# Round three's scatters without the copies that tie them to VectorE's newest result

## The chip, the cores and the metric

One core of a Trainium2 chip runs the whole kernel. The metric is the time of one execution on the device, in microseconds (us), as the median of several runs. A profile is one execution more, taken with the hardware profiler; its own time stands beside its span in the table below, since it is not the median.

## The reference, cut to what matters

There are B = 16 graphs of N = 1024 nodes with D = 128 features, and one adjacency matrix for each graph (about 8 neighbours a node). Two residual layers are computed:

```
h = relu(layernorm(x));  x = x + attention(h, adj)            # layer 0
h = relu(layernorm(x));  x = x + gnn(h, dilate(adj))          # layer 1

gnn:   h1 = bn(relu(sage(h,  adj_d, Wr1, Wx1, b1)))
       h2 = bn(relu(sage(h1, adj_d, Wr2, Wx2, b2)))
       h3 = bn(relu(sage(h2, adj_d, Wr3, Wx3, b3)))
       concat(h1, h2, h3) @ Wl + bl
sage:  out = (adj_d @ x / deg) @ Wr + x @ Wx + b;  out / norm(out)
bn:    normalised over all graphs and nodes
```

`dilate` goes through the rows of an adjacency one after another and strikes out neighbours. The batch norm needs sums over all 16 graphs, so each of the three rounds of `gnn` must be over before the next can begin.

## The kernel before, in words

**Stages.** The attention layer and the dilation run together in about the first 785 us of the span, and the dilation ends beside round one. The rows of each graph are written to DRAM in an order of their own there (indirect DMAs on GpSimd into `x2_d`), so that the few nodes that keep neighbours after the dilation stand in the first blocks. Then come three rounds of sage and batch norm over the 16 graphs, called batches here, and a fourth pass that makes the output. Round two ends before 965 us, round three (lines 1305 to 1371) runs from about 985 to 1132.5 us of the span, and round four, the pass that makes the output (lines 1374 to 1439), ends at about 1213 us.

**Order of work.** The program is written out by hand: instructions go to each engine's queue in the order in which Python issues them, and each engine works its queue in order. A `Clock` delays what belongs behind a matmul: `later(n, fn)` issues `fn` n ticks later. `in_turn` (line 1163) takes one piece of a named part, ticks the clock, and calls a function `beside`, which in rounds three and four is `pace_scatters`.

**Round three, for each batch b, in eight ticks** (mix, thirds, mix, mix, thirds, mix, turn, turn; in the last batch the thirds come last):
- `mix` (line 1029) is the sage. PE multiplies into two PSUM halves `po` (lines 1038, 1056, 1063, 1087, 1091), ScalarE squares them into `sq` (L1072), VectorE sums the squares (L1075) and bounds them (L1097), ScalarE takes the root (L1098), VectorE the reciprocal (L1101) and multiplies the halves into the first 128 columns of each row of `y` (L1104).
- `thirds` (line 1327) are the first two thirds of the final product: PE multiplies h1 and h2 into `pt` (L1332, L1333), VectorE adds the residual (L1131) and writes the sum into the last 128 columns of `y`. For the batches of `STAY` it goes to `rows_z` instead.
- `turn` (line 1109), for the batch before: PE transposes (L1114), ScalarE applies relu (L1126), VectorE collects the batch norm's statistics (L1123).

**The scatters.** The 11 batches that are not in `STAY = (2, 5, 8, 11, 14)` must go back to the order of the nodes. `scatter_rows` (line 1337) puts eight scatters of a batch, 128 rows each, on the list `waiting`, due two ticks after the batch is issued. `pace_scatters` (line 1295) issues at most one of them per tick, and none in every sixth tick. A scatter (line 571) is an indirect DMA that GpSimd (POOL) issues (L573), with a no-op behind it (L576). `y` comes from a pool of three buffers. SP, which issues the plain DMAs, brings each batch back three batches later with two loads of 512 KB (`load_back`, L1325), into the tiles that held h1 and h2 of that batch; ahead of them in each batch stands the load of x for a later batch (L1247), in two buffers. At the end of the round, the clock is flushed and what still waits is issued without the copy.

**The copies.** Before a scatter is issued in round three, while `marked` is true, `pace_scatters` issues a copy of one column of 128 values into the tile `mark`, on POOL too. Its source, `last[0]`, is the result that VectorE was issued last: a sum of squares in `nrm` (set in L1076), a column of `stats` (L1124), or the sum in `y` or in `r` (rows_z) (L1132). Nothing reads `mark`. The copy makes POOL, and so the scatter behind it, wait until VectorE has come that far.

**Round four** goes through the batches in an order that begins with one of `STAY` and then takes two of the others, five times, and ends with 15. It transposes what came back (L1380, L1385), multiplies with the third weight (L1394), adds a row (L1402), adds to `rows_z` (L1131), and stores: the 11 by a plain DMA (L1410), the five of `STAY` by eight scatters each to the output (L1387), which go through the same list. It sets `marked` to False first (L1433).

Of the kernel before, what the change touches and what calls it, by code (L numbers as in the profile page):

```python
# [533 lines left out]
@with_exitstack  # L534
def gnn_kernel(ctx: ExitStack, tc: tile.TileContext, a, out):
    nc = tc.nc
    with tc.tile_pool(name="verdict", bufs=1) as vp:
        flag = fast(tc, a, out, vp)
        bad = nc.values_load(flag[0:1, 0:1])
    tc.strict_bb_all_engine_barrier()  # L540
    with tc.If(bad > 0):
        general(tc, a, out)
# [3 lines left out]
def fast(ctx: ExitStack, tc: tile.TileContext, a, out, vp):  # L546
# [684 lines left out]
    with big:  # L1231
# [58 lines left out]
        rows_r = lambda b: blocks(r2[b // 2][:, b % 2, :])  # L1290
        rows_z = lambda b: blocks(r1[b // 2][:, b % 2, :])
        mark = few.tile([P, 1], F32, name="mark")
        waiting, ticks3, marked = [], 0, True

        def pace_scatters():

# [136 lines left out]
        marked = False  # L1433
# [591 lines left out]
```

## Time and profile before

| | |
|---|---|
| median of three runs | 1218.25 us (1217.69 to 1220.84) |
| profiled execution, its own time | 1223.52 us |
| span of that execution | 1221.7 us |
| mean granted PE clock | 0.961 of full speed |
| PE busy | 1067.6 us (87% of the span) |
| VectorE (DVE), ScalarE (ACT), GpSimd (POOL) busy | 846.0, 727.2, 575.2 us |
| scatters of round three (L573, `y_d<-y,nodes`) | 88, 86.3 us, 981 ns each |
| copies into the mark (L1302) | 81 |
| chain of work that ended last, by engine | PE 58%, DVE 16%, ACT 10%, issue 4%, POOL 4%, DMA 3% |

How to read it: the page gives the busy time of each engine over the whole span, and the share of an engine says little about one stage. For a stage there is a table by stretches of time: for each stretch its length, then for each engine the busy time in us and the number of instructions (in brackets with an x), then the granted PE clock, the busy share of the DMA engines and the rate. "PEld" is the loading of weights into PE, which goes on beside its matmuls. A row of the waits reads "who waits <- whom it waits for: total us, how many, us of the longest". A row of the timeline gives the start (us), the duration, the engine, the line, the operation, and output<-input; in square brackets stands the idle time of the engine just before, and what released it. "remote" is a releaser that the profile can't name, "issue" an idle time in which the engine waited for nothing that the profile shows.

### The profile page before, as it was taken

The numbers are of one execution on the slowest core, as the hardware profiler recorded it, in microseconds if no ns is written. First come the engines' busy times: TensorE is split into PE (matmuls) and PEld (weight loads), VectorE is DVE, ScalarE is ACT, GpSimd is POOL, SyncE is SP. The second block draws the span as 40 slices with busy tenths as digits, with TensorE's granted clock in tenths as the row PEclk, the third lists the DMA queues.
The fourth block names the chain that finished last, engine by engine and source line by source line (L and its number), as shares of the span: only waits on it lengthen the run. The fifth ranks groups of instructions, "written<-read, shape, count | busy, mean of one in ns | idle before, by whom it ended". The sixth has DMA issues, their size and how long they took to land.

```text
span 1221.7 us, 22431 instructions
## 1 busy us (share of the span) xinstructions
PE 1067.6 (87%) x7731; PEld 826.8 (68%) x7731; DVE 846.0 (69%) x2611; ACT 727.2 (60%) x1771; POOL 575.2 (47%) x1063
## 2 busy tenths in 40 slices
PE   8899989989989989989999998789779887878693
PEld 3567666766666766666666676678769877878583
DVE  7757647578867657867877988679878755556331
ACT  5677866877767767766777762468758522222120
POOL 0321742842733634554446344789401056665563
PEclk9999999999999999999999999899989999898796
DMA  7445244244344344344443421334000046665542
GB/s 233 128 145 141 86 141 145 93 141 139 99 128 140 111 131 124 119 122 118 116 131 105 126 84 38 106 82 114 19 18 1 3 145 199 186 194 164 164 144 84
DMA packets 135355, 143.77 MB, mean 118 GB/s; under 512 B 25920, under 2 KB 111296, under 8 KB 135232
## 3 DMA queue, kind: packets, MB, share of 16 engines
q1 hardware_dynamic: 123328, 111.10, 32.0%
q0 software_dynamic: 11904, 31.15, 7.8%
q8 instruction: 62, 1.02, 0.3%
q14 instruction: 61, 0.50, 0.1%
HBM read 113.71 MB, written 28.51 MB: 116 GB/s over the span
## 4 chain that ended last, share of the span: by engine, by line
PE 58%; DVE 16%; ACT 10%; issue 4%; POOL 4%; DMA 3%; another core or an unknown queue 3%; POOLq 0%; DVEq 0%; ACTq 0%
PE po L757 13%; PE ps L741 12%; PE pm L720 5%; PE po L1056 4%; PE po L1394 3%; DMA st<-in_adj_dram 3%; DVE e L744 2%; ACT e L743 2%; PE pt L1114 2%; PE pm L728 2%; PE pd L200 2%; POOL x_d L573 2%; PE pt L1332 2%; PE pt L1333 2%
## 5 line engine op out<-in xcount | busy, mean ns | idle before, releaser
L757 PEld LDWEIGHTS po<-vw,e 128*128 128x128 f32 x2048 | 270.8, 194 | 58.4 <-issue 58.2
L757 PE MATMUL po<-vw,e 128*128 128x129 f32 x2048 | 304.8, 284 | 0.0
L744 DVE TENSOR_TENSOR e<-e,ab 128x512 f32<-128x512 f32 x256 | 177.7, 694 | 156.6 <-ACT e L743 147.0
L741 PE MATMUL ps<-qT,kT 128*128 128x512 f32 x512 | 269.9, 609 | 0.6 <-ACT kT L721 0.6
L743 ACT ACTIVATE e<-ps 128x512 f32<-128x512 f32 x256 | 153.4, 600 | 94.7 <-PE ps L741 88.1
L174 ACT ACTIVATE ab<-st,d_one_k 128x1024 bf16<-128x1024 f32 x126 | 145.6, 1155 | 26.9 <-DMA st<-in_adj_dram 26.8
L573 POOL DMA_INDIRECT x_d<-xt,slot x128 | 142.9, 1116 | 39.3 <-issue 33.0
L191 ACT ACTIVATE junk<-st 128x1024 bf16<-128x1024 f32 x112 | 118.6, 1059 | 0.0
L313 POOL DMA_INDIRECT rows<-in_adj_dram,row x15 | 17.2, 1147 | 177.3 <-DVE junkv L206 82.1
L573 POOL DMA_INDIRECT y_d<-y,nodes x88 | 86.3, 981 | 22.5 <-issue 18.0
L605 POOL TENSOR_SCALAR ln_t<-ln_st 128x8 f32<-128x8 f32 x31 | 11.1, 357 | 177.4 <-DVE ln_st L598 172.2
L1072 ACT ACTIVATE sq<-po 128x512 f32<-128x512 f32 x48 | 28.5, 597 | 97.8 <-remote 39.3
L766 ACT ACTIVATE o<-po,recips 128x128 f32<-128x128 f32 x128 | 46.6, 367 | 64.1 <-DVE recips L764 59.4
L741 PEld LDWEIGHTS ps<-qT,kT 128*128 128x128 f32 x512 | 78.5, 193 | 3.6 <-ACT kT L721 1.7
L1056 PE MATMUL po<-ws,r 128*128 128x128 f32 x512 | 69.0, 277 | 3.7 <-issue 3.6
L1056 PEld LDWEIGHTS po<-ws,r 128*128 128x128 f32 x512 | 65.9, 194 | 6.3 <-issue 5.2
L617 POOL TENSOR_SCALAR hn<-xt,ln 128x128 f32<-128x128 f32 x120 | 65.0, 553 | 3.2 <-ACT e L743 1.1
L206 DVE SCALAR_TENSOR_TENSOR junkv<-pd,ab 128x64 bf16<-128x64 int32 (+7 forms) x128 | 57.4, 448 | 12.5 <-PE ps L741 6.7
L1332 PE MATMUL pt<-ws,r 128*128 128x128 f32 x224 | 48.6, 302 | 16.4 <-DVE y L1131 11.4
L728 PEld LDWEIGHTS pm<-w_L_gnn_Wo,hn 128*128 128x128 f32 x256 | 34.7, 201 | 35.2 <-ACT hn L721 22.1
L617 POOL TENSOR_SCALAR hn<-xt 128x128 f32<-128x128 f32 x112 | 54.4, 496 | 8.1 <-PE pt L627 7.2
L1131 DVE TENSOR_TENSOR r<-r,po 128x512 f32<-128x512 f32 x32 | 21.1, 685 | 52.5 <-remote 30.6
(346 smaller groups left out, 2485.5 us busy)
## 6 DMA issues: line engine op xcount, KB each, us to landing
st<-in_adj_dram SPq DMA_DIRECT2D x126, 512.0 KB
r<-y_d SPq DMA_DIRECT2D x22, 512.0 KB
xt<-x_d SPq DMA_DIRECT2D x16, 524.0 KB
x<-x_d SPq DMA_DIRECT2D x16, 512.0 KB
xt<-in_x_dram SPq DMA_DIRECT2D x15, 512.0 KB
out_dram<-r SPq DMA_DIRECT2D x11, 512.0 KB
x_d<-xt,slot POOLq DMA_INDIRECT x128
y_d<-y,nodes POOLq DMA_INDIRECT x88
```

The lines of the kernel that those rows point to most:

```text
L174: nc.scalar.activation(ab[:, k, :], st, AF.Exp, bias=self.one_k, scale=ONE_K, accum_out=self.deg[:, b, k:k + 1])
L191: nc.scalar.activation(junk(), st, AF.Exp, scale=-ZERO_K, accum_out=zeros)
L573: d = nc.gpsimd.indirect_dma_start(out=dst, out_offset=bass.IndirectOffsetOnAxis(ap=slots, axis=0), in_=src, in_offset=None)
L617: engine.tensor_scalar(hn[:, k, :], xt[:, k, :D], minus[:, k // 2, k % 2, None], rstd[:, k // 2, k % 2, None], op0=OP.add, op1=OP.mult)
L720: nc.tensor.matmul(pp, w, hT[:, 512 * g:512 * g + 512], start=True, stop=True)
L728: nc.tensor.matmul(pp[:, k, :], vT[:, j * P:(j + 1) * P], wo, start=True, stop=True)
L741: nc.tensor.matmul(p, K[b][:, k * P:(k + 1) * P], Q[b][:, c], start=True, stop=True)
L743: later(1, lambda: nc.scalar.activation(e, p, AF.Exp))
L744: later(2, lambda: nc.vector.tensor_mul(e, e, AB_[b][:, k, c]))
L757: nc.tensor.matmul(po[:, q % 2, :], E[k][:, i * P:(i + 1) * P], V[b][:, k, :], start=(k == 0), stop=(k == NB - 1))
L1056: nc.tensor.matmul(po[:, i, :], hT[:, c:c + P], wxk, start=(i == 3), stop=False)
L1332: nc.tensor.matmul(pz[:, i, :], column(r1, b, g, i), wl0, start=True, stop=False)
```

## The change: the flag of round three is False from the start

```diff
         mark = few.tile([P, 1], F32, name="mark")
-        waiting, ticks3, marked = [], 0, True
+        waiting, ticks3, marked = [], 0, False
 
         def pace_scatters():
```

The condition in `pace_scatters` is never met any more, so the copy (L1302) is not issued in round three either. Everything else is issued in the same order on every engine. A scatter then waits only for what it reads, its rows of `y`, and for its DMA queue. The first scatter of a batch waits for VectorE's multiplication into `y` (L1104), and the other seven find that done. Where the waits between the engines' instructions were placed for the copies, they go: those of VectorE's L1075 and ScalarE's L1098 for POOL, since no copy reads their tiles now.

## The prediction

> **What bounds the kernel now.** I read the page first (parts 4 and 5), then the busy time by stage, then the waits of round three, then its timeline. [...]By stage:
> ```profile
> core 0: us, PE busy (x) PEld busy (x) DVE busy (x) ACT busy (x) POOL busy (x), PEclk, DMA share, GB/s
> 930.00:965.00 35.00, 34.99 (x291) 33.41 (x291) 31.16 (x64) 27.79 (x118) 2.99 (x7) 1.00 0.01 1
> 985.00:1132.50 147.50, 118.69 (x924) 113.42 (x922) 84.66 (x166) 39.28 (x92) 94.16 (x161) 0.94 0.61 179
> ```
> Round two has no scatters, and PE never pauses (34.99 of 35.00). Round three has them, and PE is idle for 147.50 - 118.69 = 28.8 us. POOL works 94.16 us, DVE 84.66, and the DMA share is 0.61: none is full. So PE's order bounds the round, lengthened by 28.8 us of waits, and the question is what they wait for. The waits of the same stretch:
> ```profile
> ACT sq L1072 <- remote: 39.3, 7, 6.7
> POOL mark L1302 <- DVE y L1131: 24.4, 6, 6.3
> DVE y L1131 <- remote: 15.7, 4, 5.8
> PE pt L1332 <- DVE y L1131: 11.4, 3, 4.5
> ```
> POOL's mark waits for DVE, PE waits for DVE, and DVE and ACT wait for something that the profile can't name. The timeline shows one such place:
> ```profile
> 1032.70 0.39 PE L1091 MATMUL po<-ws,hr 128*128 128x128 f32 x2
> 1036.01 0.98 POOL L573 DMA_INDIRECT y_d<-y,nodes  x1 [0.16 <-issue]
> 1037.98 0.69 DVE L1131 TENSOR_TENSOR y<-x,pt 128x512 f32<-128x512 f32 x1 [5.81 <-remote]
> 1038.13 0.60 ACT L1072 ACTIVATE sq<-po 128x512 f32<-128x512 f32 x1 [6.74 <-remote]
> 1038.72 0.80 PE L1332 MATMUL pt<-ws,r 128*128 128x128 f32 x2 [4.54 <-DVE y L1131]
> 1043.19 0.18 POOL L1302 COPY mark<-y 128x1 f32<-128x1 f32 x1 [6.20 <-DVE y L1131]
> ```
> By the program DVE's L1131 and ACT's L1072 wait here for PE alone, and the matmuls that they need were started before 1033.1 (L1091 at 1032.70). Yet both go on only at 1038, 1.0 us after the last of a row of scatters ended on POOL (1036.99). The same pair of stalls stands at 1057.8, 1069.4, 1099.1 and 1119.1, each 0.9 to 1.0 us after the last scatter of a row. So while POOL issues scatter after scatter, PE's results reach the other engines late; the row stops, they arrive. And POOL stopped because its next mark waited for DVE (6.20 us), which waited for PE. The marks close a loop: they end the row of scatters that starves PE.
>
> **How long rows behave.** With a row of scatters called a train, five stretches, the fourth of round four, where nothing is marked:
> ```profile
> 986.40:998.50 12.10, 11.06 (x97) 10.79 (x96) 6.47 (x13) 2.66 (x6) 10.57 (x18) 1.00 0.34 99
> 998.50:1003.65 5.15, 1.79 (x9) 1.07 (x8) 3.27 (x8) 1.28 (x3) 3.47 (x6) 1.00 0.64 211
> 1026.50:1038.70 12.20, 7.59 (x64) 7.33 (x64) 5.64 (x12) 2.64 (x8) 9.20 (x15) 0.99 0.72 217
> 1159.20:1170.50 11.30, 9.98 (x78) 8.95 (x77) 2.75 (x4) 1.22 (x3) 7.62 (x8) 1.00 0.43 127
> 1193.30:1207.00 13.70, 3.88 (x15) 2.59 (x15) 0.69 (x1) 0.60 (x1) 8.60 (x9) 0.70 0.14 49
> ```
> A train of 8 costs PE 12.20 - 7.59 = 4.6 us at 1026, and 1.3 us at 1159. A train of 12 (986.39 to 1002.49) costs 1.0 us in its first 12.1 us and 3.4 us in the last 5.15. A train of 16 (1184.45 to 1204.34) costs nothing until 1193.30 (PE 8.90 of 8.90 us) and then nearly all: 15 matmul records in 13.70 us, single ones 0.7 or 1.4 us apart where 0.11 is normal:
> ```profile
> 1197.88 0.27 PE L1394 MATMUL po<-ws,hT 128*128 128x128 f32 x1 [1.01 <-issue]
> 1198.59 0.27 PE L1394 MATMUL po<-ws,hT 128*128 128x128 f32 x1 [0.44 <-issue]
> ```
> The train of 16 at 1132.50 to 1152.56 does the same from 1145. Length is what hurts: beyond some 9 to 12 us PE crawls until about 1 to 3 us after the train's end.
>
> **The change, part by part.** (a) 81 copies of the mark leave POOL (25 + 24 + 17 + 15 in the view of the tile mark; the last 7 of the 88 scatters have none). With a mark, scatters follow each other every 1.36 us (1014.14, 1015.50, 1016.86); without, every 1.26 us (1140.24, 1141.50). That shortens POOL by 81 x 0.10 = 8 us, none of it on the path, since POOL is idle for 53 of the 147.5 us.
> (b) POOL's waits at the mark go: 24.4 us on L1131 of y, 3.5 on L1131 of r, 2.3 on L1075. The program of after has only one wait for DVE left per batch, at its first scatter, for the scale (L1104) that completes y; the other seven wait for their queue's lane alone.
> (c) DVE and ACT lose the waits for POOL that kept a tile which a mark still had to read: 1.2 us in one place. I take nothing for it: DVE is idle for 63 us.
> (d) Buffers: by the program of after, batch 4 takes batch 1's buffer and waits for its scatters, where before it took that of batch 2 (never scattered) and batch 5 waited. Likewise 7, 10 and 13. The scatters of two batches take 16 x 1.265 + 1.2 (landing) = 21.4 us from the first y, and that buffer is wanted three batches later. PE's 118.69 / 16 = 7.4 us a batch make 22.3 us, so it is free 0.9 us before; if PE is late, by more. Nothing, then, with 0.9 us as the cover.
> (e) SP's transfers that bring y back (L1325) and the loads of x behind them keep their order and start when scatters land, not later than now. The DMA share of 0.61 leaves room.
> (f) What moves: trains. Batches to be scattered come in pairs (0,1), (3,4), (6,7), (9,10), (12,13), and 15 alone. The second y of a pair is done one batch, 7.3 us, after the first (L1104 at 1010.86 and 1018.20), and the first's eight scatters take 10.1 us. So POOL finds the second batch ready and runs 16 in one train of 20.2 us, five times. Now the marks cut each pair: 2 + 7 and 7 + break, or 8 and 8.
>
> The cost of a 16-train to PE is what the trace does not show for round three. Below: two unmarked trains of 8 would cost 2 x 1.3 = 2.6 us; a train can't give PE time, so nothing below zero. Above: 1184.4 to 1207.0 took 22.6 us for 8.90 us of work and 15 x 0.11 = 1.7 in the crawl, 12.0 us lost. Nearest in kind (same matmuls, same rows of y) is the train of 12: 1.0 us in the first 12.1, then 65% lost (3.36 of 5.15); with 21.4 us to the landing that is 1.0 + 0.65 x 9.3 = 7.1 us. But its scatters had marks between them. I take 9, between 7.1 and 12.0.
>
> Now to the sum. The eight trains of 7 to 12 scatters in round three lose 4.35 + 1.70 + 4.61 + 3.49 + 2.29 + 1.72 + 4.61 + 0.94 = 23.7 us of the 28.8 (stretch less PE busy, each by the stage view); 5.1 us lie elsewhere and stay. After: 118.7 + 5 x 9 + 5.1 = 168.8 us against 147.5: +21.3 us. The profiled execution took 1223.52 us (span 1221.7), 0.4% over the median of 1218.25; so 1244.8 profiled, and **1239.6 us** as a median. Break-even is a loss of (147.5 - 118.7 - 5.1) / 5 = 4.7 us per train.
>
> [...]
>
> **Rivals.** Longer trains starve PE more (my forecast, 0.77): 1239.6, from 7.1 to 12 us per train 1230 to 1255.
> Faster (0.17): what starves PE is not length; the marks' loop, POOL waiting for DVE and DVE for PE, is itself what keeps PE's results back. Then a train of 16 costs as two unmarked ones of 8, 2.6 us: 118.7 + 13.2 + 5.1 = 137.0, -10.5 us, 1207.8. For it: four of the eight bad trains end exactly at a marked wait, and 1159 is cheap. Against: 1145 and 1193 are bad with no mark in them.
> No change (0.06): the loss goes with the number of scatters (28.8 us over the 80 in the round), which stays; pairs only shift it. 1218. For it: trains of 8 and 12 both lose 0.1 to 0.6 us per scatter. Against: the 12-train loses three quarters in its last third.
> That the copies go but POOL is held anyway, by the lanes' waits of eight scatters back, would also give no change; round four's 1.26 us cadence excludes it.
>
> **How the numbers follow.** The range takes the forecast's own spread and reaches down towards the other cases: 1212 to 1257; I leave out most of the faster case and a little above. A measurement of this kernel can tell about 0.3%, 3.7 us, from nothing: faster 0.17, same 0.06, slower 0.77.
>
> **What would show it.** In the profile of after: five unbroken trains of 16 scatters 1.26 us apart; in the second half of each, single PE matmuls with 0.4 to 1.8 us of "issue" before them and DVE and ACT "remote" waits over 6 us; PE busy share of round three near 70%, not 80%; its length 160 to 180 us; round four as now. Wrong if PE is busy over 85% in those trains, or if the trains break at the second y because DVE itself is late (then trains of 8 stay and little changes).

## The result: 3% slower, and the profile after

| | before | after |
|---|---|---|
| median of 4 runs each | 1219.0 us (1217.69 to 1220.84) | 1257.63 us (1251.96 to 1259.98) |
| ratio | | 1.0304 (1.0274 to 1.0335) |
| profiled execution, its own time / span | 1223.52 / 1221.7 us | 1256.6 / 1254.8 us |
| granted PE clock, mean | 0.961 | 0.936 |
| round three, from its first multiplication into y to the statistics of its batch norm (L1139) | 985.0 to 1133.2: 148.2 us | 990.0 to 1172.4: 182.4 us |
| from there to the end | 88.5 us | 82.4 us |

The spans differ by 33.1 us: 5.0 us of it lie before round three (which the change doesn't touch), 34.2 us in round three, -6.1 us in round four. The direction was forecast, and 21.3 us where the medians are 38.6 us apart. The time itself lies 0.6 us above the range; the ratio of 1.0304, put on the 1218.25 us that the forecast started from, makes 1255.3 us, just inside it.

The busy times of round three, first of the kernel before, in a stretch that ends at the same instruction as that of after:

```profile
core 0: us, PE busy (x) PEld busy (x) DVE busy (x) ACT busy (x) POOL busy (x), PEclk, DMA share, GB/s
985.00:1133.20 148.20, 118.89 (x926) 113.63 (x925) 85.33 (x166) 39.98 (x93) 94.86 (x161) 0.94 0.61 178
```

and of the kernel after:

```profile
990.00:1172.40 182.40, 133.81 (x927) 125.30 (x928) 84.97 (x167) 41.18 (x93) 78.61 (x82) 0.80 0.53 151
```

Two things grew. PE's idle time went from 29.3 us (148.20 - 118.89) to 48.6 us (182.40 - 133.81). And PE was busy 14.9 us longer with the same number of matmuls (926 and 927 records), at a granted clock of 0.80 in place of 0.94. The waits of that stretch, after:

```profile
POOL y_d L573 <- DVE y L1104: 96.2, 5, 32.2
DVE r L1131 <- remote: 62.5, 5, 14.7
ACT sq L1072 <- remote: 56.6, 4, 14.7
PE pt L1332 <- issue: 19.8, 19, 1.7
PE pt L1333 <- issue: 12.6, 16, 1.5
```

POOL waits five times for the scaling of a y (L1104), and each time it then issues the 16 scatters of a pair of batches in one row (the trains of the prediction); batch 15 makes a row of 8 at the end. VectorE and ScalarE wait up to 14.7 us at a time for something without a name, where it was at most 6.7 us; and PE now has idle times of up to 1.7 us in these lines in which it waits for nothing that the profile shows. The timeline of the third row (1061.1 to 1081.0), from its middle on, with POOL and PE alone (weight loads left out):

```profile
1069.94 0.96 POOL L573 DMA_INDIRECT y_d<-y,nodes  x1 [0.30 <-issue]
1071.07 0.38 PE L1063 MATMUL po<-pc,rows_of 128*128 128x512 bf16 x1 [0.96 <-issue]
1071.21 0.96 POOL L573 DMA_INDIRECT y_d<-y,nodes  x1 [0.30 <-issue]
1071.28 0.27 PE L1332 MATMUL pt<-ws,r 128*128 128x128 f32 x1
1072.48 0.96 POOL L573 DMA_INDIRECT y_d<-y,nodes  x1 [0.31 <-issue]
1073.18 0.27 PE L1332 MATMUL pt<-ws,r 128*128 128x128 f32 x1 [1.63 <-issue]
...
1075.28 0.60 PE L1332 MATMUL pt<-ws,r 128*128 128x128 f32 x2 [1.61 <-issue]
```

The scatters start 1.27 us apart without a break, and from the seventh on PE gets through no more than three matmuls a scatter, sometimes none. Three of the five rows, each to 1 us past its last scatter, and then the stretch behind each of the five, up to the point where the clock is whole again:

```profile
991.50:1012.60 21.10, 13.12 (x96) 12.52 (x94) 6.82 (x14) 2.67 (x6) 15.55 (x16) 0.84 0.48 147
1061.00:1082.00 21.00, 12.74 (x85) 10.85 (x83) 5.91 (x12) 2.75 (x6) 15.40 (x16) 0.82 0.56 167
1135.60:1156.50 20.90, 12.47 (x82) 10.77 (x80) 5.91 (x12) 2.79 (x6) 15.36 (x16) 0.75 0.76 217
```
```profile
1012.60:1019.80 7.20, 6.01 (x26) 5.80 (x27) 4.08 (x8) 1.86 (x5) 0.00 (x0) 0.53 0.27 84
1045.80:1051.00 5.20, 4.18 (x22) 4.15 (x22) 3.00 (x7) 2.47 (x6) 0.00 (x0) 0.55 0.07 9
1082.00:1087.00 5.00, 3.29 (x16) 3.57 (x17) 2.65 (x4) 1.67 (x3) 0.00 (x0) 0.50 0.02 3
1119.30:1125.00 5.70, 4.75 (x21) 4.31 (x21) 3.58 (x8) 2.50 (x6) 0.00 (x0) 0.50 0.12 20
1156.50:1162.00 5.50, 4.40 (x20) 4.40 (x21) 2.96 (x6) 1.87 (x4) 0.00 (x0) 0.50 0.69 181
```

The three cost PE 8.0, 8.3 and 8.4 us of idle time, the other two, read in the same way, 8.3 and 8.5: 41.5 us in all. Then comes what I had not counted: the clock. For 5 to 7 us behind each row PE works at about half of it, and inside the rows the mean is 0.75 to 0.84. Eight matmuls of L1056 take 1.91 us behind the first row (at 1014.75) and 1.06 us elsewhere (at 1066.99).

### The profile page after: what moved, and what is told of

Its sections match the earlier page's. It is cut to its first block, busy times and chain, and to the rows that moved or that the text cites. A ratio compares the mean times of both kernels' runs of the same rounds, so it can differ in the third digit from the quotient of the medians.

```text
span 1254.8 us, 22272 instructions
## 1 busy us (share of the span) xinstructions
PE 1085.9 (87%) x7731; PEld 841.6 (67%) x7731; DVE 846.8 (67%) x2611; ACT 729.6 (58%) x1771; POOL 557.8 (44%) x982
## 4 chain that ended last, share of the span: by engine, by line
PE 62%; DVE 15%; ACT 9%; issue 6%; POOL 3%; DMA 3%; another core or an unknown queue 1%; SPq 0%; POOLq 0%; DVEq 0%; ACTq 0%
PE po L757 13%; PE ps L741 12%; PE pm L720 5%; PE po L1056 5%; PE pt L1114 3%; DMA st<-in_adj_dram 3%; PE pt L1332 3%; PE pt L1333 3%; PE po L1394 2%; DVE e L744 2%; ACT e L743 2%; PE pd L200 2%; PE pm L728 2%; ACT ab L174 2%
## 5 line engine op out<-in xcount | busy, mean ns | idle before, releaser
L174 ACT ACTIVATE ab<-st,d_one_k 128x1024 bf16<-128x1024 f32 x126 | 145.6, 1155 | 25.4 <-DMA st<-in_adj_dram 19.6
L605 POOL TENSOR_SCALAR ln_t<-ln_st 128x8 f32<-128x8 f32 x31 | 11.1, 359 | 178.5 <-DVE ln_st L598 171.2
L1056 PE MATMUL po<-ws,r 128*128 128x128 f32 x512 | 72.1, 283 | 7.3 <-issue 7.3
L1056 PEld LDWEIGHTS po<-ws,r 128*128 128x128 f32 x512 | 68.4, 200 | 8.1 <-issue 6.8
L1332 PE MATMUL pt<-ws,r 128*128 128x128 f32 x224 | 51.0, 305 | 25.8 <-issue 19.8
L1333 PE MATMUL pt<-ws,r 128*128 128x128 f32 x224 | 50.9, 305 | 12.9 <-issue 12.6
L1332 PEld LDWEIGHTS pt<-ws,r 128*128 128x128 f32 x224 | 40.8, 216 | 29.0 <-issue 22.4
```

What stands on the lines that cost most here:

```text
L174: nc.scalar.activation(ab[:, k, :], st, AF.Exp, bias=self.one_k, scale=ONE_K, accum_out=self.deg[:, b, k:k + 1])
L1056: nc.tensor.matmul(po[:, i, :], hT[:, c:c + P], wxk, start=(i == 3), stop=False)
L1332: nc.tensor.matmul(pz[:, i, :], column(r1, b, g, i), wl0, start=True, stop=False)
L1333: nc.tensor.matmul(pz[:, i, :], column(r2, b, g, i), wl1, start=False, stop=True)
```

## The experiments

Theory: scatters issued by POOL in one unbroken row hold back PE, the more the longer the row; the copies helped because each could wait, and so broke the rows. The rivals: the copies help as such (an instruction between two scatters, a slower cadence); the close tie to VectorE's order helps; the traffic to memory is what hurts; a busy POOL is. Each group below ran on one chip, with runs of the kernel before on the same chip, and only ratios are compared across groups. The runs of the result are the first group; their chip may be that of the second or the third. Round three is given here from the second L1139 to the third, before and after:

```profile
970.10:1133.20 163.10, 130.92 (x1008) 124.89 (x1009) 95.39 (x193) 43.36 (x102) 95.05 (x162) 0.94 0.58 168
974.20:1172.40 198.20, 146.86 (x1009) 137.58 (x1010) 94.88 (x194) 44.43 (x102) 78.61 (x82) 0.80 0.51 144
```

### Second group: the kernel before takes 1229.36 us

**A copy without a tie.**
```diff
-                    nc.gpsimd.tensor_copy(mark, last[0])
+                    nc.gpsimd.tensor_copy(mark, eps)
```


> The kernel before, with the copy into the mark ahead of each scatter of round three taken from a constant tile: 81 copies and the cadence of 1.36 us stay, only the wait for VectorE's newest result is gone. By my theory (PE is starved by long unbroken rows of scatters, and the mark's wait is what breaks them) five rows of 16 come, each with about 8 us of idle PE, and the time is that of the kernel after, 1250 to 1260 us. By the rival that the copies themselves help (a POOL instruction between two scatters, or the slower cadence), it stays near 1219 us.

Measured: 1251.35 us, ratio 1.0208 (1.0154 to 1.0262). By the ratios a third of the loss is gone, two thirds stay. Round three and its third row:

```profile
974.30:1167.70 193.40, 153.01 (x995) 139.53 (x1010) 95.72 (x193) 43.98 (x102) 95.94 (x162) 0.80 0.51 148
1059.42:1081.93 22.51, 15.47 (x98) 13.93 (x100) 7.32 (x14) 3.31 (x7) 18.94 (x32) 0.76 0.51 155
```

The copies are there, the rows of 16 too. This one costs 7.0 us (22.51 - 15.47), the five 6.1 to 7.0, 6.6 in the mean, and the round's clock is 0.80 again. So the copy as an instruction helps a little (8.3 - 6.6 = 1.7 us a row), and the wait in it does the rest.

**A tie at every fourth scatter.**
```diff
-                if marked:
+                sent += 1
+                if marked and sent % 4 == 1:
```


> The kernel before, with the copy from VectorE's newest result ahead of every fourth scatter only. By my theory a tie every 5 us still breaks a row as soon as PE, and so VectorE, is held back, and rows stay at about 8: 1212 to 1228 us. By the rival that each single tie matters (it keeps POOL from running more than one result ahead), most of the gain is lost: 1240 us or more.

Measured: 1242.58 us, ratio 1.0103 (1.0047 to 1.0159). The time alone would be the rival's; but this chip is 10 us slower with the kernel before, and by ratio the result lies between the two (at most 1.008 and at least 1.018, on the 1218.25 us of the kernel before in the first group). The lengths of the rows tell why: three of its rows ran to 12 before a tie stopped them. One row of 12, and one of 8 with the row of 4 that came 0.9 us behind it:

```profile
1024.38:1040.47 16.09, 8.14 (x69) 7.79 (x68) 5.22 (x11) 2.23 (x6) 11.97 (x14) 0.89 0.62 193
1092.48:1103.40 10.92, 9.24 (x72) 8.03 (x71) 5.31 (x11) 2.57 (x6) 8.21 (x11) 1.00 0.52 161
1103.28:1109.06 5.78, 0.75 (x3) 0.30 (x2) 0.00 (x0) 0.00 (x0) 3.86 (x4) 0.68 0.27 95
```

The first two cost PE 8.0 and 1.7 us, and a row of 4 at 1046.9, with nothing close ahead of it, 0.05 us: the price by length that the theory asks for. The row of 4 shown cost 5.0 us, so a break of 0.9 us doesn't end the effect of the row ahead of it. That a tie every 5 us is enough was wrong.

**A fixed pause, no tie.**
```diff
+                def send(k):
+                    if k == 0:
+                        for _ in range(8):
+                            nc.gpsimd.tensor_scalar(recips.rearrange("p b k -> p (b k)"), identf, 1.0, 0.0, op0=OP.mult, op1=OP.add)
+                    scatter(y_d[b], nodes[:, b, k:k + 1], y[:, k, :], f"y_{b}")
```
(`send(k)` takes the place of the scatter on the list)

> The kernel after (no ties), with eight POOL operations of 128x128 on tiles that nobody else uses, some 4 us together, ahead of the first scatter of each batch. Rows of 16 become two of 8 with a fixed pause. By my theory (length of the row) PE is released in each pause and a row of 8 costs 1 to 5 us as in the kernel before: 1210 to 1230 us. By the rival that it is VectorE's order or the time at which the buffers of y come free that costs, the pause only makes POOL later: 1257 us or more.

Measured: 1227.62 us, ratio 1.0004 (0.9982 to 1.0025). Eight of POOL's own operations took 3.0 us, and with them alone the whole loss is gone, without one tie to VectorE. A pair of batches is now two rows, costing 2.5 and 1.2 us here and 0.8 to 2.6 in the other pairs:

```profile
1022.46:1033.32 10.86, 8.34 (x70) 8.05 (x70) 6.01 (x12) 2.59 (x6) 8.51 (x11) 1.00 0.81 236
1035.74:1046.60 10.86, 9.63 (x70) 9.07 (x69) 5.03 (x10) 2.07 (x5) 8.51 (x11) 0.89 0.82 241
```

**Plain stores by SP.**
```diff
-                for k in range(NB):
-                    waiting.append((ticks3 + 2, lambda k=k: scatter(...)))
+                later(2, lambda: nc.sync.dma_start(y_d[b].rearrange("(k p) d -> p k d", p=P), y))
```


> The kernel after, with each batch's eight scatters in round three replaced by one plain store of the same 1 MB, issued by SP. This leaves out the permutation of the rows of the 11 batches, so the output of these is in another order. By my theory it is POOL's issuing of scatters that starves PE and not the traffic: round three falls to PE's own work and the 5 us elsewhere, 118.7 + 5.1 = 124 us, so 1190 to 1200 us in all. By the rival that the traffic to memory and back starves PE, round three stays as long as before or after: 1219 to 1257 us.

Measured: 1183.86 us, ratio 0.9658 (0.9615 to 0.9702). Round three without a scatter:

```profile
972.70:1096.70 124.00, 119.07 (x995) 117.15 (x1010) 93.66 (x193) 43.19 (x102) 0.00 (x0) 0.97 0.79 222
```

The DMA share is higher than in either kernel (0.79), and PE is idle for 4.9 us of 124.0. The traffic doesn't hold PE back. The round is as long as expected, the whole a little shorter (1190 to 1200 us was expected). PE was also busy for 11.9 us less than in the kernel before, at a clock of 0.97 in place of 0.94: the rows of that kernel had a price in PE's work too.

### Third group: the kernel before takes 1228.82 us

**Ties in round four too** (the line `marked = False` at L1433 is taken out).

> The kernel before, with the copies from VectorE's newest result in round four too (the flag stays True). By my theory the two rows of 16 in round four, which cost PE 12 and some 8 us, are broken as well: 10 us less, ratio to the kernel before 0.985 to 0.997. By the rival that in round four POOL has no slack and any wait of POOL makes the last scatters later, the ratio is 1.00 to 1.01.

Measured: 1228.07 us, ratio 0.9991 (0.9965 to 1.0017): no gain, a miss of mine. The ties didn't break the rows. One of 13 stayed where the rounds meet and one of 15 in round four, here the latter:

```profile
1169.07:1190.10 21.03, 15.42 (x102) 13.40 (x103) 5.00 (x8) 2.50 (x5) 17.43 (x29) 0.85 0.40 122
```

This one cost 5.6 us, that of 13 from 1134.0 on 9.4. The marks of round four waited only 11.1 us for VectorE. I take it that POOL runs behind there, so that the result a copy asks for is old by the time POOL comes to it; no run showed that by itself.

**Short pauses ahead of every fourth scatter, in rounds three and four.**
```diff
+                    if k % 4 == 0:
+                        for _ in range(4):
+                            nc.gpsimd.tensor_scalar(recips..., identf, 1.0, 0.0, op0=OP.mult, op1=OP.add)
```
(the same ahead of the scatters of L1387)

> The kernel after (no ties), with four POOL operations on unused tiles (some 1.5 us) ahead of every fourth scatter in rounds three and four. With a pause of 3 us ahead of every eighth in round three alone the ratio to the kernel before was 1.00. By my theory PE is released in each pause, and rows of 4 cost less than rows of 8; round four's rows of 12 and 16 go too: ratio 0.98 to 0.995. By the rival that a pause must be longer than some 2 us to release PE, rows of 16 with short gaps act as rows of 16: 1.01 to 1.03.

Measured: 1208.47 us, ratio 0.9851 (0.9801 to 0.99): on this chip it beats the kernel before by 1.5%, and no other version that does the whole work did in any group. Round three, a pair of rows of 4, and the end of round four:

```profile
967.20:1112.30 145.10, 126.74 (x995) 123.03 (x1010) 94.27 (x194) 43.78 (x102) 98.90 (x155) 0.93 0.62 186
1024.06:1036.31 12.25, 11.88 (x103) 11.60 (x103) 7.55 (x15) 3.15 (x7) 9.75 (x15) 1.00 0.75 233
1163.37:1195.93 32.56, 0.00 (x0) 0.00 (x0) 1.02 (x2) 0.00 (x0) 24.18 (x36) 0.54 0.24 75
```

In this pair of rows eight scatters cost PE 0.4 us. Others of the round cost up to 2.6 us; the fourth group shows that this isn't the crawl. The last line is the price: PE has no matmul left in these 32.6 us, while POOL issues its last 20 scatters. In round four the pauses make POOL the bound.

**Plain DMAs issued by POOL, and a busy POOL without DMAs.**
```diff
-                    ... scatter(y_d[b], nodes[:, b, k:k + 1], y[:, k, :], f"y_{b}")
+                    ... nc.gpsimd.dma_start(y_d[b][k * P:(k + 1) * P, :], y[:, k, :])
```


> The kernel after, with each scatter of round three replaced by a plain DMA of the same 128 rows, still issued by POOL (it leaves out the permutation of the 11 batches' rows). By my theory what starves PE is POOL's issuing of a DMA in one unbroken row, indirect or not: the ratio stays at 1.02 to 1.04. By the rival that it is the indirect form (reading the list of rows), it falls to the 0.966 of the plain stores by SP.

In the other kernel three operations like those of the pauses take the place of each scatter, and SP stores y as above.

> The kernel with plain stores by SP (the permutation left out), with three POOL operations of 128x128 (some 1.1 us) in the place of each scatter, so that POOL is about as busy as with the scatters but issues no DMA. By my theory POOL's own work costs PE nothing: the ratio stays at 0.966, within 0.01. By the rival that a busy POOL as such [...] holds the others up, it rises to 1.00 or more.

Measured: 1185.41 us, ratio 0.9647 (0.9588 to 0.9706), and 1182.33 us, ratio 0.9622 (0.9566 to 0.9678). Round three took 123.7 and 123.9 us. So a busy POOL (67.7 us of it) costs PE nothing, and 88 plain DMAs that POOL issued cost nothing either. The longest row of these, 16 in 8.6 us, and a row of 16 scatters in round four of the same execution:

```profile
998.07:1007.69 9.62, 9.57 (x86) 9.55 (x86) 7.43 (x16) 3.81 (x10) 8.62 (x16) 1.00 0.64 200
1125.07:1146.09 21.02, 12.24 (x83) 10.61 (x85) 4.17 (x7) 2.27 (x4) 15.32 (x16) 0.82 0.33 100
```

The plain ones cost PE 0.05 us, the scatters 8.8. So the number of DMAs in a row is not what counts. But a plain DMA takes POOL 0.53 us, not 0.96, and most rows of a batch lasted 4.25 us: the form isn't yet parted from the time that the row lasts.

### Fourth and fifth group, on two other chips: the kernel before takes 1154.9 and 1156.75 us

The next kernels were to shorten the pauses and to settle the form.

**Pauses in round three only, of four operations and of two** (as above, without the part in L1387).

> The kernel after with a pause of four POOL operations (1.5 us) ahead of every fourth scatter in round three only. With the same pauses in round four too the ratio was 0.985, and there PE sat idle for the last five rows because POOL was late. By my theory round three keeps its 145 us and round four ends 5 to 8 us earlier: ratio 0.975 to 0.985. By the rival that round four's rows of 16 then starve PE again for as much as the pauses cost: 0.985 to 0.995.

> The same with half the pause (two POOL operations, 0.75 us; scatters of two rows of four about 1.1 us apart instead of 1.8). If it takes only a gap of about 1 us to let PE's results through, POOL has more room and the ratio is 0.97 to 0.98. If a gap must be longer than some 1.5 us, rows join to long ones and the ratio goes back to 1.00 to 1.02, near that of the copies from a constant, whose gap of 0.45 us at every scatter gave 1.021.

**Plain DMAs of 64 rows issued by POOL.**
```diff
+                        nc.gpsimd.dma_start(y_d[b][k * P + h * 64:k * P + h * 64 + 64, :], y[p, k, :])
```


> Plain DMAs issued by POOL in the place of the scatters, as before with the permutation left out, but each of 64 rows, so that there are 16 for each batch and POOL issues for some 17 us in one row for a pair of batches; with 8 of 128 rows a pair took only 8.5 us, and the ratio was 0.965. By the theory that it is the indirect form that starves PE, the ratio stays at 0.965. By the rival that any unbroken issuing of DMAs by POOL beyond some 8 to 10 us does, it rises to 1.00 or more.

Measured: 1176.19 us, ratio 1.0204 (1.0154 to 1.0255); 1161.65 us, ratio 1.0076 (1.0054 to 1.0097); 1145.85 us, ratio 0.9921 (0.989 to 0.9953). No ratio is the one that my theory expected, and none of this answers what was asked, for the kernel before itself takes 74 us less on this chip than in the two groups above. Here is round three and one row of 44 scatters in round four, in the kernel with the longer pauses:

```profile
954.30:1099.00 144.70, 127.22 (x1009) 122.84 (x1010) 94.10 (x193) 43.20 (x102) 98.96 (x154) 0.93 0.62 187
1110.38:1166.66 56.28, 38.93 (x322) 36.35 (x320) 19.76 (x29) 10.43 (x18) 42.17 (x44) 0.88 0.61 180
```

In an unbroken row of 44 scatters, 55 us long, PE does 322 matmul records; at 1193 in the kernel before it did 15 in 13.70 us. PE waits once in that row, 1.0 us for ScalarE (L1391), which waits 15.1 us for the scattered rows; from 1150.3 on it has no matmul left. No scatter of this row holds PE back. A pause then only makes POOL later, and VectorE waits 26.6 us in the round for buffers of y that are still being scattered (L1131). The round itself is the same as with the same pauses in the third group (144.7 and 145.1 us, PE busy 127.2 and 126.7), and with plain DMAs it takes 124.1 us here and 123.7 there. So in round three the chips differ only where long rows of scatters run.

**A pacing of its own for each pair of batches** (the pair (0,1) unbroken, the others as the expectation says).

> The kernel after, with another pacing for each pair of batches in round three, read from the trace pair by pair: (0,1) unbroken; (3,4) 0.75 us of POOL's own work ahead of every fourth scatter; (6,7) plain DMAs of 64 rows issued by POOL (it leaves out the permutation of these two batches); (9,10) 0.37 us ahead of every second scatter; (12,13) 1.5 us ahead of every eighth. If this chip is like the first ones: by my theory the unbroken pair costs PE 7 to 9 us of idle time, the pair with a pause ahead of every fourth under 4 us, that ahead of every eighth 2 to 5 us. By the rival that the gap must be longer than 1.5 us, all three scatter pairs cost 6 us or more. If it is the indirect form that starves PE, the pair of plain DMAs costs under 1 us; if any DMA issued by POOL does, 4 us or more. If this chip is like the last one, where no row of scatters held PE back at all, no pair costs over 2 us and the kernel before takes some 1155 us.

Measured in the fifth group: 1158.76 us, ratio 1.0026 (1.0008 to 1.0044). This chip is like the fourth group's, as the last sentence of the expectation has it. The unbroken pair:

```profile
972.51:993.60 21.09, 20.93 (x183) 20.86 (x185) 15.17 (x31) 7.19 (x17) 16.13 (x18) 1.00 0.64 199
```

PE is idle for 0.16 us in a row of 16, where the kernel after lost 8.0 us in the same row, with the same scatters, 0.96 us each and about 1.27 us apart. Two of the pairs with pauses, (3,4) and (9,10), cost 2.0 and 1.1 us.

## Why the prediction was right, and where it fell short

**The rows, step (f).** Right. Five rows of 16 came, 20.0 us each, for the reason given: the second y is ready before the first's eight scatters are over. I had taken 9 us of idle time for each, a choice between two rough readings; it was 8.3. Idle time elsewhere in the round was taken as 5.1 us and was 48.6 - 41.5 = 7.1. Together: idle time forecast 50.1 us (45 + 5.1), measured 48.6.

**The term of the sum that was mis-sized** is "118.7" in "118.7 + 5 x 9 + 5.1": PE's own work was taken as fixed, and it measured 133.8 us. Most of the difference is the clock, and the 118.7 already held a part of it. In round three of before PE had about half the clock in five stretches of 3.4 us, 17 us with 16.9 us of work in them; in that of after in six of 6.8 to 17.1 us, 72 us with 41.9 us of work, in the rows and behind them. One of each:

```profile
1038.50:1041.90 3.40, 3.18 (x15) 3.18 (x16) 3.24 (x9) 1.57 (x5) 0.00 (x0) 0.52 0.61 156
1036.90:1050.60 13.70, 7.34 (x28) 6.45 (x28) 3.07 (x6) 2.07 (x5) 6.04 (x7) 0.50 0.20 69
```

If half of the work at half the clock is loss, that is an estimated 8.4 us before and 20.9 after: 12.5 of the 14.9 us. What the other 2.4 are is not shown; a matmul on its own counts as 0.27 us of work, where in an unbroken series they follow each other every 0.11.

The granted clock is 0.52 and 0.50 in these two stretches, and 1.00 between two rows of after (1051 to 1061). A forecast from the five stretches of before would hardly have moved: with one of 3.4 us to each row it takes as many as the 118.7 already holds, an estimated 5 x 3.4 / 2 = 8.5 us. What the five rows brought is longer stretches: in the second half of a row PE does little more than single matmuls, and the clock is not whole again until 5 to 7 us behind it.

**Steps (a), (b), (c).** Right. Cadence 1.27 us, one named wait per row, no wait of VectorE for POOL. **Step (d), the buffers:** right; VectorE doesn't wait for rows of y in the waits of after. **Step (e):** no engine waits for a load in the same view. **Round four "as now":** it became 6.1 us shorter. Before, the last eight scatters of y joined the first eight of the output to a row of 16; after, they are two rows of 8 (from 1170.6 and from 1182.3).

**The rivals.** Faster, because the marks' loop is itself what keeps PE's results back: refuted in the second group by the constant copies, which wait for nobody and still lose 2%. No change, because the loss goes with the number of scatters: refuted by the pauses, where eight scatters cost 0.4 us.

**Round three without scatters.** PE's own work and the 5.1 us that lie elsewhere make 118.7 + 5.1 = 123.8 us. That is what the kernels without scatters there took (124.0, 123.7 and 123.9 us), so the plain DMAs and POOL's own arithmetic in their place added nothing to it. Rows of 16 scatters did hold PE back in the first three groups, by 8.0 to 8.5 us each in the kernel after.

**What stays open.** Why the chips differ: no view shows a difference but its effect, and each chip was used at one time only, so chip and moment aren't parted. By stages (before in the first group, the kernel with the shorter pauses in the fourth), the attention stage, which has indirect DMAs too, takes 744.0 and 728.0 us, round one 119.1 and 120.6, round two, which has no scatters, 74.0 and 73.9. What PE waits for in its "issue" times is not shown either. So it is shown that long unbroken rows of scatters cost PE its time on some chips, but not through what. Whether the indirect form or the time that a row lasts is decisive wasn't settled either, since the long rows of plain DMAs fell on chips without the effect, and had short gaps. The kernel after wasn't run on the chips of the last two groups; the pair that costs 0.16 us suggests that it loses nothing there. Nor was the version that wins in the third group; with the same pauses in round three alone, the fourth loses 2%. So no version was found that is best on both kinds of chip.

## What to carry to other kernels

A wait that looks like pure cost can be the brake that ends a harmful stretch: before taking one out, ask what the engine will do with the freedom, and look for places where it already runs free (round four showed the price). If a pace is what is needed, set it: a fixed pause between short rows of indirect DMAs did as well as the ties in the second group (ratio 1.0004), and better in the third, when the rows were of four (0.9851); on a chip without the effect it cost 2% (1.0204). And look at the clock beside the idle PE time: here the five rows cost 41.5 us as idle time, and the half clock in them and behind them an estimated 12.5 us more than before. Work that is taken from a profile as fixed can hold such stretches already. Last, run the kernel before beside every experiment: without it the fourth group would have looked like a gain of 4%.

## What the runs showed of the hardware

- In the first three groups PE crawls in the second half of an unbroken row of indirect DMAs issued by POOL. In round three, read to 1 us past a row's end, it was idle for 0.05 us at most in a row of 4 that stands alone (ties at every fourth scatter), 0.8 to 3.9 in rows of 8, 4.2 to 8.0 in those of 12, 8.0 to 8.5 in those of 16 of the kernel after. A break of 0.9 us didn't end it (5.0 us idle in the row of 4 behind it); with pauses of 1.5 us ahead of every four, eight scatters cost 0.4 us in the pair shown. On the two chips of the last groups it didn't crawl: 0.16 us idle in a row of 16, 322 matmul records in a row of 44. The kernel before takes 1219 to 1229 us in the former and 1155 to 1157 in the latter, and round two, which has no scatters, took 74.0 us in the first group and 73.9 in the fourth.
- Neither plain DMAs issued by POOL (0.53 us each, rows of up to 8.6 us) nor POOL's own arithmetic (67.7 us in the round) held PE back: 123.7 and 123.9 us for round three.
- In the second half of each of the five rows of 16 of the kernel after, PE's granted clock fell to about half (0.50 and 0.51 in the six stretches of 6.8 to 17.1 us), and it was so (0.50 to 0.55) for 5 to 7 us after the row. Eight matmuls of L1056 took 1.91 us there and 1.06 us elsewhere.
